# A two-layer graph network on one core: layer two's sums in three wider products, and every 64th gather replaced by single-row loads from SP

## The chip, the cores and the metric

The kernel runs on one core of a Trainium2 chip. The core has TensorE (PE; its weight loads are shown as PEld), VectorE (DVE), ScalarE (ACT), GpSimd (POOL) and SyncE (SP), which run their own instruction streams and wait for one another through semaphores. SP, ACT and POOL also issue DMAs, which 16 DMA engines carry out. The metric is the device time of one execution in microseconds (us); lower is better. Times of single instructions come from one profiled execution.

## The reference

The inputs are 6,250 nodes with 160 features each (64 scalars and 32 three-vectors), and 200,000 edges (src, dst), sorted by dst. There are two layers, each followed by a residual and a layer norm. Cut to what matters, with constants and reshapes left out:

```
# layer one, per edge: ss, vv = features of src; e0, e1 = edge attributes (1 + 3)
out0 = ss*e0 @ W1 + dot(vv, e1) @ W2
out1 = (ss @ W3) x e1 + (vv*e0) @ W4 + cross(vv, e1) @ W5
m_agg = segment_sum(concat(out0, out1), dst)
x1 = layernorm(x + (x + relu(linear(m_agg))))

# layer two: w = relu(edge_attr_10 @ W_fc1) @ W_fc2   (192 a edge: w0 64, w1 64, w2 32, w3 32)
l0, l1 = linear(x1);  y0, y1 = l0[src], l1[src]
m0 = w0*y0*e0;  m1 = (w1*y0) x e1;  m2 = (w2*e0) x y1;  m3 = w3*dot(y1, e1)
s0..s3 = segment_sum(m0..m3, dst)
o0 = s0 @ W_l2_00 + s3 @ W_l2_10;  o1 = s1 @ W_l2_01 + s2 @ W_l2_11
x2 = layernorm(x1 + self_interaction(x1) + 0.5*(o0, o1))
```

## The kernel before, in words

**Tiles.** The edges are cut into 391 chunks of 512, a chunk into four tiles (J = 4) of 128 edges, one edge a partition. Because edges are sorted by dst, the edges of one chunk end in a window of at most W = 40 neighbouring nodes. Per chunk the kernel builds a 0/1 matrix of edges by window places (`oh`, L290) and multiplies it with the four edge attributes (`S`, L294: 128 edges x 4 tiles x 4 attributes x 40 places). A matmul of the edges' features with S then sums messages by node into a window of PSUM (`ab`), and DVE adds that window into accumulators in SBUF at a start read from a register (`add`, L356 to L378; the addition itself is L367). The accumulators are accA (4 groups of node columns) and accB (one).

**Gathers.** The features of a tile's 128 source nodes are gathered from a table in HBM by one indirect DMA of GpSimd (`gathered`, L128), four a chunk, 1,564 a layer: from x in layer one, from ytab in layer two. They land in g, a pool of GRING = 8 chunks; the first two chunks are gathered ahead into a pool of their own.

**Layer one.** ScalarE copies 32 of the features four times side by side (`repeat`, L331), and PE makes two products a tile: 128 features by the 160 columns of S (L350), and the copies by the same 160 columns (L353). When all edges of a block of 128 nodes are done (`closing`), the block is projected (L390), normed, projected again (L452, L453) and written to ytab and btab (L460, L464).

**Layer two.** `hidden` (L300, L303) makes 100 hidden values per edge from `et`, which SP loads every second chunk (L260). `message` (L314 to L326) makes the weights w in PSUM and multiplies them with the gathered features into m, 320 columns an edge. `matmuls` (L337 to L345) makes three products a tile over these columns: the first 128 by 40 columns of S, the next 128 by 160, the last 64 by 80, so 280 columns in all. They fill seven windows of `ab`, of which some are not used. `add` then takes five additions: 128 rows by 40, 64 by 120, 64 by 80, and twice 32 by 40. A finished block is projected with wc (L476), whose rows are laid out to fit the accumulators (L221 to L231), added to the base that SP loads (L469), normed and sent out by SP (L487).

**Order.** The order on every engine is the order in which the program issues it. A loop over t (L496) calls each stage for chunk t minus its lag, so for layer two:

```
stages = [(load, 0), (onehot, 1), (hidden, 1), (message, 2), (matmuls, 3), (add, 4)]
parts = [(fetch_base, 3), (project_last, 5), (residual_last, 6), (deviation, 7), (sent, 8)]
```

Layer one has load, onehot, repeat, matmuls and add, and for a finished block fetch, project, rectify, residual, deviation, normed, turned, kept, linear and written. SP's queue holds all loads and stores but the gathers, srcs and ytab: raw (edge attributes, every 32 chunks, L275), et, xt (L415), btab, base, out and, at step PREPARE = 8 of layer one, the weights. Successive DMAs of SP and ACT use eight semaphores in turn, so a DMA waits for the one eight before it.

Of the kernel before, what the change touches and what calls it, by code (L numbers as in the profile page):

```python
# [10 lines left out]
F32 = mybir.dt.float32  # L11
BF16 = mybir.dt.bfloat16
I32 = mybir.dt.int32
AF = mybir.ActivationFunctionType
ALU = mybir.AluOpType
# [8 lines left out]
J = 4  # L24
# [16 lines left out]
GRING = 8  # L41
PREPARE = 8

# [10 lines left out]
def gnn_kernel(ctx: ExitStack, tc: tile.TileContext, x, src, dst, ea, sh, avec,  # L54
# [64 lines left out]
    with tc.If(go > 0) as both:  # L119
        windowed(tc, x, srcs, rel, low, ident, iota, ahead, ea, sh, avec, *weights, out)  # L120
# [3 lines left out]

def gathered(nc, pool, srcs, table, c):
    g = pool.tile([P, J, D], F32, name="g")
    for j in range(J):
        nc.gpsimd.indirect_dma_start(out=g[:, j, :], out_offset=None, in_=table,  # L128
                                     in_offset=bass.IndirectOffsetOnAxis(ap=srcs[:, c, j:j + 1], axis=0))
    return g  # L130
# [3 lines left out]
def windowed(ctx: ExitStack, tc: tile.TileContext, x, srcs, rel, low, ident, iota, ahead, ea, sh, avec,  # L134
# [11 lines left out]
    accA = const.tile([P, 4, NW], F32, name="accA")  # L146
    accB = const.tile([P, NW], F32, name="accB")
    eps = const.tile([P, 1], F32, name="eps")
    nc.vector.memset(eps, EPS)
    zero = const.tile([P, 4], F32, name="zero")  # L150
# [9 lines left out]
    def clear(k):  # L160
        part = accA[:, k, :] if k < 4 else accB
        nc.scalar.activation(part, zero[:, 0:1].to_broadcast([P, NW]), AF.Copy)  # L162

    def prepare(wp, wpp):
# [5 lines left out]
        nc.sync.dma_start(fc2, wfc2)  # L170
# [51 lines left out]
        nc.sync.dma_start(wc[32:96, 4, 0:M0], w00)  # L222
        for r, g, i in ((0, 4, 0), (96, 4, 1), (64, 0, 2)):
            nc.sync.dma_start(wc[r:r + 32, g, vec[i]], w11)
        for i in range(3):
            nc.sync.dma_start(wc[0:M0, 1 + i, vec[i]], w01)
        for r, g in ((96, 1), (0, 0), (32, 0)):
            nc.sync.dma_start(wc[r:r + 32, g, 0:M0], w10)
        nc.vector.tensor_scalar(wc, wc, L2_SCALE, None, op0=ALU.mult)
        for r, g in ((96, 1), (0, 0), (32, 0)):  # L230
            nc.vector.tensor_scalar(wc[r:r + 32, g, 0:M0], wc[r:r + 32, g, 0:M0], INV3, None, op0=ALU.mult)  # L231

    def sums(layer, table, gp, hp, sp):
        with ExitStack() as s:
# [13 lines left out]
            G, S, SH, ET, H, M, PA, AT, RAW = {}, {}, {}, {}, {}, {}, {}, {}, {}  # L248

            def load(c):  # L250
                if layer or c not in ahead:
                    G[c] = gathered(nc, gp, srcs, table, c)
                else:
                    G[c] = ahead.pop(c)
                if c % 2 == 0 and layer:
                    n = min(2, NCH - c)
                    et = ET[c // 2] = xp.tile([P, 2, CH // 2], F32, name="et")
                    part = ea[:, c * CH:(c + n) * CH].rearrange("f (c h e) -> f c h e", c=n, h=2)
                    for r in range(2):
                        nc.sync.dma_start(et[64 * r:64 * r + 10, :n, :], part[:, :, r, :])  # L260
                if c == 0:
                    attributes(0)
                if c % 32 == 12:
                    attributes(c // 32 + 1)

# [41 lines left out]
            def message(c):  # L307

                m = M[c] = wp.tile([P, J, 320], F32, name="m")
                h = H.pop(c)  # L310
                for q in range(0, J, 2):
                    pw = pp.tile([P, 2, 192], F32, name="pw")
                    for j in range(2):
                        nc.tensor.matmul(pw[:, j, :], h[:, q + j, :], fc2, start=True, stop=True)  # L314
                    y = G[c][:, q:q + 2, :]
                    thirds = m[:, q:q + 2, 0:288].rearrange("p j (d u) -> p j d u", d=3)
                    nc.vector.tensor_tensor(  # L317
                        thirds[:, :, 0:2, 32:96], pw[:, :, 0:128].rearrange("p j (a u) -> p j a u", a=2),
                        y[:, :, None, 0:64].to_broadcast([P, 2, 2, 64]), op=ALU.mult)
                    y1 = y[:, :, 64:160].rearrange("p j (d u) -> p j d u", d=3)  # L320
                    nc.vector.tensor_tensor(  # L321
                        thirds[:, :, :, 0:32], y1,
                        pw[:, :, None, 128:160].to_broadcast([P, 2, 3, 32]), op=ALU.mult)
                    nc.vector.tensor_tensor(  # L324
                        m[:, q:q + 2, 224:320].rearrange("p j (d u) -> p j d u", d=3), y1,
                        pw[:, :, None, 160:192].to_broadcast([P, 2, 3, 32]), op=ALU.mult)  # L326
# [7 lines left out]
            def matmuls(c):  # L334
                one = S.pop(c)
                if layer:
                    t = M.pop(c)  # L337
                    ab = PA[c] = pa.tile([P, 7, W], F32, name="ab")
                    parts = [(ab[:, 4, :], slice(0, 128), slice(0, 1)),
                             (ab[:, 0:4, :], slice(128, 256), slice(0, 4)),  # L340
                             (ab[0:64, 5:7, :], slice(256, 320), slice(2, 4))]
# [14 lines left out]
            def add(c):  # L356
# [8 lines left out]
                def into(rows, k, part):  # L365
                    v = accA[rows, k, ds(at, W)] if k is not None else accB[rows, ds(at, W)]
                    nc.vector.tensor_tensor(v, v, part, op=ALU.add)  # L367

                if layer:
                    into(slice(0, 128), None, ab[:, 4, :])  # L370
                    into(slice(0, 64), slice(1, 4), ab[0:64, 1:4, :])
                    into(slice(64, 128), slice(0, 2), ab[64:128, 0:2, :])
                    for i in range(2):
                        into(slice(32 * i, 32 * i + 32), 0, ab[32 * i:32 * i + 32, 5 + i, :])
                else:
                    into(slice(0, 128), slice(0, 4), ab[:, 0:4, :])
                    for k in range(4):
                        into(slice(32 * k, 32 * k + 32), None, ab[32 * k:32 * k + 32, 4 + k, :])  # L378
# [6 lines left out]
            def projected(name, pool, weights, b):  # L385
                r = rows(b)
                po = T[name, b] = pool.tile([P, D], F32, name=name)
                for g in range(5):
                    lhs = accA[:, g, b * P:b * P + r] if g < 4 else accB[:, b * P:b * P + r]
                    nc.tensor.matmul(po[:r], lhs, weights[:, g, :], start=(g == 0), stop=(g == 4))  # L390
# [29 lines left out]
            def rectify(b):  # L420
# [3 lines left out]
                nc.scalar.activation(accA[:, :, b * P:b * P + r], zero[:, :, None].to_broadcast([P, 4, r]), AF.Copy)  # L424
                nc.scalar.activation(accB[:, b * P:b * P + r], zero[:, 0:1].to_broadcast([P, r]), AF.Copy)
# [45 lines left out]
            def project_last(b):  # L471
                r = rows(b)
                po = T["po", b] = pl_.tile([P, D], F32, name="po")
                for g in range(5):
                    lhs = accA[:, g, b * P:b * P + r] if g < 4 else accB[:, b * P:b * P + r]
# [13 lines left out]
            if layer:  # L489
                stages = [(load, 0), (onehot, 1), (hidden, 1), (message, 2), (matmuls, 3), (add, 4)]  # L490
                parts = [(fetch_base, 3), (project_last, 5), (residual_last, 6), (deviation, 7), (sent, 8)]
            else:
                stages = [(load, 0), (onehot, 1), (repeat, 1), (matmuls, 2), (add, 5)]
# [408 lines left out]
```

## Time and profile before

| | us |
|---|---|
| runs: median of 3 (lowest, highest) | 5196.45 (5195.57, 5202.86) |
| the profiled execution's own time | 4000.83 |
| its span, first to last instruction | 3999.1 |
| layer one's gathers, first to last start | 11.0 to 1979.6 |
| layer two's gathers, first to last start | 2005.9 to 3965.8 |
| busy: PE, PEld, DVE, ACT, POOL | 3469.6, 2900.8, 2516.1, 601.9, 2972.9 |
| mean granted clock of TensorE | 0.931 of full speed |

The profiled execution is much shorter than the runs; durations of instructions are from it alone. In the lines that follow, a group of instructions is named by its source line, engine, operation and tiles (out<-in), then its count, then busy time and the mean of one in ns, then the idle time of the engine before them and what ended it. A wait is put down to whatever released it last; "issue" is time in which nothing that the profile shows was waited for. A q behind an engine's name means its queue, so that SPq is the time in which SP issues a DMA. Matmuls overlap, so PE's busy share says less than the spacing of the matmuls' starts.

### The profile page before, as it was taken

How to read it: one execution, taken by the hardware profiler on the slowest of the kernel's cores; microseconds unless marked ns; L12 is line 12 of the kernel's file. 1: busy time of each engine (PE TensorE's matmuls, PEld its weight loads, DVE VectorE, ACT ScalarE, POOL GpSimd, SP SyncE). 2: the span in 40 equal slices, each digit the busy share in tenths (PEclk: the TensorE clock that was granted, in tenths of full speed). 3: DMA queues.
4: the chain of work that ended last, by engine and by line, in shares of the span. 5: the costliest groups of instructions: out<-in, count | busy, mean ns of one | idle time of the engine just before them, and what ended most of it. 6: DMA issues, size and time to landing. Idle time of an engine off the chain costs nothing.

```text
span 3999.1 us, 66393 instructions
## 1 busy us (share of the span) xinstructions
PE 3469.6 (87%) x21616; PEld 2900.8 (73%) x21617; DVE 2516.1 (63%) x8489; ACT 601.9 (15%) x1187; POOL 2972.9 (74%) x3137
## 2 busy tenths in 40 slices
PE   4777777777777777787799999999999999999999
PEld 4655655556566566665578888888888888888888
DVE  4444444444444444445567877787888888888887
ACT  3111111111111111112211111111111111111111
POOL 6777777777777777777677777777777777777775
PEclk8888888888888988889989999999999999999999
DMA  2222222222222323333222222232333333333332
GB/s 76 69 66 71 71 69 71 72 74 71 74 76 74 76 74 79 80 76 82 70 70 70 75 74 73 75 76 73 77 76 77 79 76 79 77 80 80 78 77 60
DMA packets 204128, 297.15 MB, mean 74 GB/s; under 512 B 61124, under 2 KB 150342, under 8 KB 203774
## 3 DMA queue, kind: packets, MB, share of 16 engines
q0 software_dynamic: 150144, 256.45, 26.0%
q1 hardware_dynamic: 46466, 31.56, 2.8%
q10 hardware_dynamic: 7164, 4.80, 0.4%
q8 instruction: 176, 2.88, 0.3%
q14 instruction: 178, 1.46, 0.1%
HBM read 280.57 MB, written 12.00 MB: 73 GB/s over the span
## 4 chain that ended last, share of the span: by engine, by line
PE 38%; POOL 4%; issue 4%; DVE 2%; DMA 2%; DVEq 0%; ACT 0%; ACTq 0%; POOLq 0%
PE ab L344 20%; PE pw L314 11%; PE ph L300 5%; POOL g L128 4%; DMA g<-ytab,srcs 2%; PE po L476 2%; DVE accA L367 1%; DVE S L294 0%; DVE m L317 0%; DVE oh L290 0%; DVE m L324 0%; DVE accB L367 0%; DVE m L321 0%; DVEq L367 0%; DVE sh L282 0%
## 5 line engine op out<-in xcount | busy, mean ns | idle before, releaser
L128 POOL DMA_INDIRECT g<-ytab,srcs x1564 | 1484.6, 949 | 501.6 <-issue 435.5
L128 POOL DMA_INDIRECT g<-in_x,srcs x1564 | 1484.9, 949 | 476.3 <-issue 406.2
L344 PE MATMUL ab<-S,m 128*128 128x40 f32 (+2 forms) x9384 | 1123.9, 275 | 0.1
L350 PE MATMUL ab<-S,g 128*128 128x160 f32 x3128 | 735.7, 352 | 430.1 <-DMA g<-in_x,srcs 317.4
L344 PEld LDWEIGHTS ab<-S,m 128*128 128x128 f32 (+1 forms) x9384 | 1052.8, 174 | 71.6 <-issue 67.9
L350 PEld LDWEIGHTS ab<-S,g 128*128 128x128 f32 x3128 | 529.0, 214 | 621.3 <-DMA g<-in_x,srcs 472.6
L294 DVE TENSOR_TENSOR S<-oh,sh 128x640 f32<-128x640 f32 x782 | 644.8, 825 | 365.6 <-PE ab L353 279.1
L353 PE MATMUL ab<-S,r 128*128 128x160 f32 x3128 | 660.0, 366 | 65.7 <-ACT r L331 63.2
L367 DVE TENSOR_TENSOR accA<-accA,ab 32x40 f32 (+3 forms) x1955 | 467.0, 239 | 326.1 <-ACT accA L424 177.2
L353 PEld LDWEIGHTS ab<-S,r 128*128 128x128 f32 x3128 | 551.5, 231 | 150.5 <-ACT r L331 150.1
L314 PE MATMUL pw<-fc,h 100*128 100x192 f32 x3128 | 620.2, 341 | 2.3 <-DVE m L324 2.3
L314 PEld LDWEIGHTS pw<-fc,h 100*128 100x128 f32 x3128 | 501.9, 191 | 144.3 <-issue 140.1
L317 DVE TENSOR_TENSOR m<-pw,g 128x256 f32<-128x256 f32 x782 | 328.2, 420 | 302.8 <-PE pw L314 220.7
L303 ACT ACTIVATE h<-ph 100x512 f32<-100x512 f32 x391 | 233.5, 597 | 1734.1 <-PE ph L300 1724.7
L331 ACT ACTIVATE r<-g 128x512 f32<-128x512 f32 x391 | 245.7, 629 | 1593.0 <-DMA g<-in_x,srcs 1528.1
L367 DVE TENSOR_TENSOR accB<-accB,ab 32x40 f32 (+1 forms) x1955 | 372.3, 190 | 26.0 <-ACT accB L162 5.5
L300 PE MATMUL ph<-et,fc 10*100 10x256 f32 x1564 | 267.7, 418 | 5.1 <-ACT h L303 4.2
L324 DVE TENSOR_TENSOR m<-g,pw 128x192 f32<-128x192 f32 x782 | 270.5, 346 | 0.0
L321 DVE TENSOR_TENSOR m<-g,pw 128x192 f32<-128x192 f32 x782 | 268.3, 343 | 0.0
L290 DVE TENSOR_TENSOR oh<-iota,rel 128x160 f32<-128x160 f32 x782 | 257.7, 330 | 16.9
L462 DVE SCALAR_TENSOR_TENSOR base<-pl,a_sb,z 128x160 f32<-128x160 f32 (+1 forms) x49 | 18.8, 383 | 320.1 <-ACT y L459 320.1
L300 PEld LDWEIGHTS ph<-et,fc 10*100 10x100 f32 x1564 | 99.9, 161 | 47.0 <-issue 9.2
(80 smaller groups left out, 856.2 us busy)
## 6 DMA issues: line engine op xcount, KB each, us to landing
g<-in_x,srcs POOLq DMA_INDIRECT x1564
g<-ytab,srcs POOLq DMA_INDIRECT x1564
et<-in_ea SPq DMA_DIRECT2D x390, 20.0 KB
raw<-in_sh SPq DMA_DIRECT2D x96, 64.0 KB
xt<-in_x SPq DMA_DIRECT2D x48, 80.0 KB
ytab<-y ACTq DMA_DIRECT2D x48, 80.0 KB
btab<-base SPq DMA_DIRECT2D x48, 80.0 KB
base<-btab SPq DMA_DIRECT2D x48, 80.0 KB
```

Of the source, the lines that this page charges most:

```text
L128: nc.gpsimd.indirect_dma_start(out=g[:, j, :], out_offset=None, in_=table, in_offset=bass.IndirectOffsetOnAxis(ap=srcs[:, c, j:j + 1], axi ...
L290: nc.vector.tensor_tensor(oh, iota[:, None, :].to_broadcast([P, J, W]), rel[:, c, :, None].to_broadcast([P, J, W]), op=ALU.is_equal)
L294: nc.vector.tensor_tensor(S[c], oh[:, :, None, :].to_broadcast([P, J, 4, W]), attr[:, :, :, None].to_broadcast([P, J, 4, W]), op=ALU.mult)
L300: nc.tensor.matmul(ph[:, r, 0:CH // 2], fc1[64 * r:64 * r + 10, :], ET[c // 2][64 * r:64 * r + 10, c % 2, :], start=True, stop=True)
L314: nc.tensor.matmul(pw[:, j, :], h[:, q + j, :], fc2, start=True, stop=True)
L317: nc.vector.tensor_tensor(thirds[:, :, 0:2, 32:96], pw[:, :, 0:128].rearrange("p j (a u) -> p j a u", a=2), y[:, :, None, 0:64].to_broadca ...
L321: nc.vector.tensor_tensor(thirds[:, :, :, 0:32], y1, pw[:, :, None, 128:160].to_broadcast([P, 2, 3, 32]), op=ALU.mult)
L324: nc.vector.tensor_tensor(m[:, q:q + 2, 224:320].rearrange("p j (d u) -> p j d u", d=3), y1, pw[:, :, None, 160:192].to_broadcast([P, 2, 3 ...
L344: nc.tensor.matmul(o, t[:, j, f], one[:, j, k, :], start=(j == 0), stop=(j == J - 1), skip_group_check=True)
L350: nc.tensor.matmul(ab[:, 0:4, :], t[:, j, 0:128], one[:, j, :, :], start=(j == 0), stop=(j == J - 1), skip_group_check=True)
L353: nc.tensor.matmul(ab[:, 4:8, :], r[:, j, :], one[:, j, :, :], start=(j == 0), stop=(j == J - 1), skip_group_check=True)
L367: nc.vector.tensor_tensor(v, v, part, op=ALU.add)
```

## The change

There are two parts.

**Layer two's products.** The 320 message columns are permuted: w1 with y0 comes first, then (at 160) w0 with y0, and the two sets of 96 stand at 64 and 224. To match this, fc2 is loaded in three pieces with its first two blocks exchanged, and wc is filled in another layout. The three products a tile are then 128 message columns by 120 columns of S (attributes 1 to 3), 128 by 80 (attributes 0 and 3), and 64 by 40 (attribute 0), 240 in all, and fill five windows exactly. accA and accB become one tile acc with five groups, and one addition of 128 rows by 200 takes the place of five. Layer one keeps its five additions; rectify clears with one instruction instead of two.

**Rows by SP.** In every sixteenth chunk (15, 31, ... 383) POOL issues three gathers instead of four. The last tile of that chunk is loaded by SP, one DMA for each of its 128 rows. `fetch_rows` runs first in every step t: it loads eight node numbers into SP's registers and issues eight row loads of 640 bytes for the single chunk of its group of 16 steps. `numbers` loads the 128 node numbers into one partition, half a group ahead. `place_rows` has ScalarE copy the finished tile into g at lag 1, ahead of onehot. GRING falls from 8 to 7.

```
-GRING = 8
+GRING = 7
+EVERY = 16
+ROWS = -(-P // EVERY)
...
+def single(c):
+    return c % EVERY == EVERY - 1
...
 def gathered(nc, pool, srcs, table, c):
     g = pool.tile([P, J, D], F32, name="g")
-    for j in range(J):
+    for j in range(J - 1 if single(c) else J):
         nc.gpsimd.indirect_dma_start(out=g[:, j, :], out_offset=None, in_=table,
...
-    accA = const.tile([P, 4, NW], F32, name="accA")
-    accB = const.tile([P, NW], F32, name="accB")
+    acc = const.tile([P, 5, NW], F32, name="acc")
...
-        nc.sync.dma_start(fc2, wfc2)
+        for i, f in enumerate((64, 0)):
+            nc.sync.dma_start(fc2[:, 64 * i:64 * i + 64], wfc2[:, f:f + 64])
+        nc.sync.dma_start(fc2[:, 128:192], wfc2[:, 128:192])
...
+            def numbers(c):
+                if c < NCH:
+                    NUM[c] = hp.tile([1, P], I32, name="num")
+                    nc.sync.dma_start(NUM[c], src[:, c, J - 1:J].rearrange("p a -> a p"))
+
+            def fetch_rows(t):
+                c = t - t % EVERY + EVERY - 1
+                if c >= NCH:
+                    return
+                if t == 0:
+                    numbers(c)
+                if t % EVERY == 0:
+                    ROW[c] = hp.tile([P, D], F32, name="row")
+                if t % EVERY == EVERY // 2:
+                    numbers(c + EVERY)
+                a, b = t % EVERY * ROWS, min(P, t % EVERY * ROWS + ROWS)
+                _, at = nc.values_load_multi_w_load_instructions(
+                    NUM[c][0:1, a:b], engines=[mybir.EngineType.SP], min_val=0, max_val=N - 1,
+                    skip_runtime_bounds_check_because="node numbers")
+                for i in range(a, b):
+                    nc.sync.dma_start(ROW[c][i:i + 1, :], table[ds(at[i - a], 1), :])
+
+            def place_rows(c):
+                if single(c):
+                    del NUM[c]
+                    nc.scalar.activation(G[c][:, J - 1, :], ROW.pop(c), AF.Copy)
...
-                    thirds = m[:, q:q + 2, 0:288].rearrange("p j (d u) -> p j d u", d=3)
+                    mq = m[:, q:q + 2, :]
                     nc.vector.tensor_tensor(
-                        thirds[:, :, 0:2, 32:96], pw[:, :, 0:128].rearrange("p j (a u) -> p j a u", a=2),
+                        mq.rearrange("p j (a u) -> p j a u", a=2)[:, :, :, 0:64],
+                        pw[:, :, 0:128].rearrange("p j (a u) -> p j a u", a=2),
                         y[:, :, None, 0:64].to_broadcast([P, 2, 2, 64]), op=ALU.mult)
...
-                    ab = PA[c] = pa.tile([P, 7, W], F32, name="ab")
-                    parts = [(ab[:, 4, :], slice(0, 128), slice(0, 1)),
-                             (ab[:, 0:4, :], slice(128, 256), slice(0, 4)),
-                             (ab[0:64, 5:7, :], slice(256, 320), slice(2, 4))]
+                    ab = PA[c] = pa.tile([P, 5, W], F32, name="ab")
+                    parts = [(ab[:, 0:3, :], slice(0, 128), slice(1, 4)),
+                             (ab[:, 3:5, :], slice(128, 256), slice(0, 4, 3)),
+                             (ab[64:128, 4, :], slice(256, 320), slice(0, 1))]
...
-                    into(slice(0, 128), None, ab[:, 4, :])
-                    into(slice(0, 64), slice(1, 4), ab[0:64, 1:4, :])
-                    into(slice(64, 128), slice(0, 2), ab[64:128, 0:2, :])
-                    for i in range(2):
-                        into(slice(32 * i, 32 * i + 32), 0, ab[32 * i:32 * i + 32, 5 + i, :])
+                    into(slice(0, 128), slice(0, 5), ab)
...
-                stages = [(load, 0), (onehot, 1), (hidden, 1), (message, 2), (matmuls, 3), (add, 4)]
+                stages = [(fetch_rows, 0), (load, 0), (place_rows, 1), (onehot, 1), (hidden, 1), (message, 2), (matmuls, 3), (add, 4)]
...
-                stages = [(load, 0), (onehot, 1), (repeat, 1), (matmuls, 2), (add, 5)]
+                stages = [(fetch_rows, 0), (load, 0), (place_rows, 1), (onehot, 1), (repeat, 1), (matmuls, 2), (add, 5)]
```

## The prediction

> **What bounds the kernel now.** I read the two stages first, then GpSimd's waits, then the groups with shapes kept apart, then single chunks of the timeline. First, busy time by engine in a stretch of layer one and one of layer two (columns: the stretch, its length, then PE, PEld, DVE, ACT and POOL busy with instruction counts, granted clock, DMA share, GB/s):
>
> ```profile
> 100.00:1900.00 1800.00, 1372.84 (x6451) 1086.04 (x6450) 829.81 (x2784) 298.52 (x654) 1362.22 (x1438) 0.87 0.29 74
> 2200.00:3900.00 1700.00, 1689.30 (x12563) 1470.05 (x12562) 1368.22 (x4609) 209.10 (x380) 1286.83 (x1357) 0.99 0.31 77
> ```
>
> The reader should see that POOL's rate is the same in both: 1800/1438 and 1700/1357 are 1.252 and 1.253 us a gather, although PE has a quarter of its time free in layer one and 11 us in 1700 in layer two. The 16 DMA engines are 30% busy, so bandwidth binds nothing. Next, whom POOL waits for (total us, times, longest):
>
> ```profile
> POOL g L128 <- issue: 841.6, 2681, 25.3
> POOL g L128 <- PE ab L353: 36.9, 121, 0.3
> POOL g L128 <- PE ab L350: 26.2, 86, 0.3
> ```
>
> "issue" is no wait for anybody: 841.6/2681 is 0.31 us, the ordinary space between two gathers, and the "waits" for PE are just as long. So POOL never waits for a buffer. In the trace the gathers start 1.251 us apart by median, from 11.0 to 1979.6 us and from 2005.9 to 3965.8 us; the one hole is the 26 us between the layers. A chunk of four gathers takes 5.00 us, whatever the rest does. Then layer two's own work:
>
> ```profile
> L344 PE MATMUL ab<-S,m 128*128 128x160 f32 x3128 | 527.0, 312 | 0.0
> L344 PE MATMUL ab<-S,m 128*128 128x40 f32 x3128 | 388.6, 273 | 0.1
> L344 PE MATMUL ab<-S,m 128*64 128x80 f32 x3128 | 302.5, 240 | 0.0
> L367 DVE TENSOR_TENSOR accA<-accA,ab 64x120 f32 x391 | 103.2, 264 | 0.1
> L367 DVE TENSOR_TENSOR accA<-accA,ab 128x160 f32 x391 | 122.7, 314 | 306.9 <-ACT accA L424 177.2 <-PE ph L390 119.8 <-ACT accA L162 7.8
> ```
>
> PE is nearly a second bound there. With everything ready it needs 4.784 us a chunk (median spacing of the first L314 matmul), plus about 0.16 us for the projections; that is 4.94 against POOL's 5.00. Late in layer two it lags some 15 us behind the gathers, and this lag is part of the 32 us between POOL's last gather and the end. Last, what one queue issue costs SP:
>
> ```profile
> 3027.57 0.67 SPq L260 DMA_DIRECT2D et<-in_ea  x2
> 3028.29 1.73 SPq L275 DMA_DIRECT2D raw<-in_sh  x4
> 3030.11 0.68 SPq L260 DMA_DIRECT2D et<-in_ea  x2
> 3030.84 0.35 SPq L469 DMA_DIRECT2D base<-btab  x1
> ```
>
> Each issue holds SP for 0.33 to 0.43 us, with some 0.045 us between two. Now SP has little to do; after the change it has much.
>
> **The change, part by part.**
>
> *Gathers removed.* Chunks 15, 31, ... 383 have three gathers instead of four: 24 a layer, 48 in all, x 1.251 us = 60.0 us of the bound engine (a chunk falls from 5.00 to 4.93 us on average). They lie on the path, since POOL never waits. A rule speaks against counting this: the Trainium skill's page "DMA: Bandwidth & Descriptors", section "Issuing engines are not separate DMA queues", says that spreading DMAs over issuing engines saves only the sequencer's issue time, usually small beside the DMA. By that rule the move is worth about 0. By the rows the issue time is exactly the bound, with DMA engines 30% busy; I take 60.0 us.
>
> *Rows added on SP.* 6,144 DMAs of one row, eight a chunk in both layers, each behind a register operation; and before each eight a register load. No row of the trace shows a one-row DMA with an address from a register. The nearest by number of rows is et (20 short rows, median 0.325 us), then raw (32 rows, median 0.419). A register operation is 0.076 us (DVE's at L367), a load 0.463 us (SP's at L117). With 0.045 us between each: a row is 0.325 + 0.076 + 0.09 = 0.49 us, eight are 3.93, with the load 4.45 us a chunk. Added to that, each chunk: raw, xt, btab (or base, out) and the numbers, 0.19 us; in layer two also et, two issues every second chunk, 0.37. So 4.64 us in layer one and 5.00 in layer two. The ends: with 0.25 us a DMA (the shortest issues are 0.255 to 0.28) 4.0 and 4.4; with 0.419, 5.4 and 5.75. A gain below nothing is excluded, because SP's work only grows. I take 4.64 and 5.00, by the nearest row. Against a budget of 4.93 layer one fits and layer two is over by 0.07 us, 27 us in 391 chunks. That is the closest figure in this sum.
>
> *What waits for SP.* SP issues in program order. A late row makes et, base and out late behind it. place_rows makes ACT wait for the 128 rows, and behind it on ACT stand repeat or hidden of the same chunk; PE needs these one stage later. So a lag of SP up to a stage costs nothing, and a lag that grows is paid in full. At the start the numbers and eight rows come before raw: about 7 us (two loads, 2 us of landing, eight rows) until the first S. POOL has a ring of nine chunks to fill then (45 us), so I cost this at nothing. With GRING 7 the cover is 5 us smaller; in layer one PE follows a gather within 1.5 us, in layer two within 15 us, well under 35 us. ACT gains 48 copies of 128x160 (nearest, L459: 0.378 us): 18 us of an engine 15% busy, nothing. The split of fc2 into three loads and the permuted message columns leave shapes as they are: nothing.
>
> *Matmuls.* In single chunks of layer two the L344 matmuls start 112 ns apart at 40 columns, 136 at 160 and 69 at 80 (64 weight columns), each tile in two passes: 8 x (112 + 136 + 69) = 2.54 us. At 112 the weight load of 128 columns is the limit. With 120, 80 and 40 columns: 8 x (112 + 112 + 58), 58 being half of a 128-column load, = 2.26 us. PE saves 0.28 us a chunk, 109 us in all, beside POOL's bound; PE falls to about 4.66 us with projections. What reaches the end is only the lag at the tail, some 15 us.
>
> *A slower clock.* The Trainium skill's page "TensorE: Matmul & The Clock Gate", section "HAM oscillation — how this bites in real kernels", has the clock fall to half only after idle gaps over about 3.4 us. In layer one the longest waits of PE for a gather are 2.3 us, and its granted clock is 0.87. So row and rule differ. By the rule layer two stays near 1.0; by the row 5% more idle time could bring it to 0.87, and 4.66/0.87 = 5.36 would exceed 4.93. But PE would then be busy throughout, where the clock is 0.99. I take nothing, and keep 0 to 15 us for the tail.
>
> *Additions.* Five of 1.07 us together become one of 128x200, 0.36 us (314 ns at 160 columns, 1.06 ns for each further one). DVE saves 0.7 us a chunk in layer two, where it is 80% busy and PE waits for it 2.3 us in total: nothing.
>
> **Sum** in the profiled execution: -60 for POOL, -15 for the tail, +27 for SP in layer two: about -48 with SP at its estimate, -75 if SP keeps up, and a loss at SP's upper end (the first rival). I take -60, between the first two: 4000.83 to 3941, a factor of 0.985.
>
> **The runs.** The profiled execution took 4000.83 us (span 3999.1 and 1.7 around it), the median of the three runs is 5196.45, which is 1.299 times that, and they agree within 7.3 us. Nothing in the profile shows these 1196 us. If they stretch the gathers, one takes 1.66 us, a chunk 6.64, and SP has room even at 5.75. If they are a constant, the saving is 60 of 5196. If they are a half clock of PE in layer two (two chunks at about 2150 us run at half clock and take 8.9 us instead of 4.8), PE binds there. I scale: 5196.45 x 0.985 = 5118.
>
> **The rivals.**
>
> *SP becomes the bound (slower).* Mechanism: SP's chunk exceeds POOL's, in layer two first, where et stands behind the rows. At the profiled pace the loss equals the gain at 5.12 us a chunk, a row DMA of only 0.34 us. At 0.419 us: 391 x (5.75 - 4.93) + 391 x (5.4 - 4.93) = 504 us, less 75, so +430; half of that way, +140 to +200. For it: raw's 0.419, and the wait of every DMA for the one eight before it. Against: et's 0.325, and the pace of the runs, where 5.75 fits in 6.64. About 5335, between 5210 and 5600.
>
> *PE binds in the runs (faster by more).* At half clock the saving doubles to 0.56 us a chunk; over 391 chunks 219 us: about 4980. For it: half clock makes a chunk 8.9 us, and 3198 us left for layer two would be 8.2 us each. Against: layer two is granted 0.99 in the profile.
>
> *Nothing gained.* SP eats just what POOL saves: 5186 to 5207.
>
> **How the numbers follow.** POOL's saving, SP keeping up or nearly: 0.49, 5070 to 5150, likeliest 5118. PE bound: 0.11. Nothing gained: 0.06. SP bound: 0.34. About 0.2% (10 us) is what these runs can tell from no change. Faster 0.60, same 0.06, slower 0.34. The range leaves out most of the PE case (0.08) and the far part of SP's (0.12): 5020 to 5380. The likeliest case alone is 5070 to 5150.
>
> **What would show it.** Right: 3,080 gathers, still 1.25 us apart and without holes; L344 near 2.3 us a chunk; SP's eight rows and load under 4.9 us; ACT's waits at place_rows short. Wrong: gathers of POOL with waits for a buffer, ACT waiting long for row, PE waiting for et or ACT in layer two; then SP binds. A time below 5020 would mean that PE bound the runs.

## The result: 5872 us, slower by 13%

| | us |
|---|---|
| changed kernel, median of 4 runs (lowest, highest) | 5872.31 (5853.35, 5877.98) |
| kernel before beside it, median of 4 runs | 5196.20 |
| ratio, with its 95% interval | 1.1291 [1.1263, 1.132] |
| profiled execution of the changed kernel: own time, span | 5877.98, 5876.1 |
| its gathers, first to last start: layer one, layer two | 11.8 to 2981.9, 3020.4 to 5826.7 |

The forecast was 5118 us (5020 to 5380) and faster; the measured time lies above the range and on the other side. One thing has to be known to read the numbers below: the kernel before takes about 4.0 ms in the profile shown before and in set B (one chip), and 5.1 to 5.2 ms in the measured runs and in sets A, C and D (two other chips), so every ratio below compares runs on one chip.

The two stages of the changed kernel, busy time by engine (columns as before: stretch, length, then PE, PEld, DVE, ACT and POOL busy with counts, clock, DMA share, GB/s):

```profile
100.00:2900.00 2800.00, 1296.13 (x6578) 1168.58 (x6578) 849.18 (x2863) 306.25 (x650) 1366.65 (x1443) 0.70 0.19 48
3100.00:5700.00 2600.00, 2189.81 (x13419) 1913.95 (x13418) 1189.45 (x3461) 231.20 (x425) 1362.56 (x1422) 0.80 0.21 53
```

2800/1443 and 2600/1422 are 1.94 and 1.83 us a gather instead of 1.25. In layer one PE is busy for less than half of the stretch, POOL too; so a wait ends last there, and none of these engines is full. Who waits for whom (total us, times, longest), from the waits of the changed kernel:

```profile
...
ACT g L300 <- DMA row<-in_x: 938.1, 24, 59.8
POOL g L135 <- DVE acc L402: 845.8, 226, 8.7
...
PEld ab L385 <- ACT g L300: 700.0, 24, 45.0
...
DVE z L460 <- DMA xt<-in_x: 408.2, 25, 31.8
...
POOL g L135 <- ACT r L366: 276.8, 32, 35.6
...
PE ph L336 <- DMA et<-in_ea: 147.2, 49, 36.7
```

All 24 copies of `place_rows` in layer one wait, 39 us each (938.1/24), PE stands behind them (700 us), and POOL, whose ring is then full, waits for ACT (276.8 us). POOL's 845.8 us for DVE are all in layer two, and most of them do not come from the rows: at this pace the kernel before has 673.2 us of such waits (b0), and the products without rows 654.9 (mm). The lines with `xt` and `et` are loads that stand in SP's queue behind the rows. SP itself waits for little, some 80 us in layer one and 310 in layer two, most of the latter before its `out` stores (L517):

```profile
SPq L517 <- DVE oh L326: 147.6, 28, 19.7
SPq L517 <- DVE z L440: 104.0, 17, 19.7
SPq L295 <- DMA row<-ytab: 42.9, 86, 1.4
```

What SP's instructions take: L291 is the load of eight numbers, L295 the rows (count: shortest/median/longest in ns, first and last start):

```profile
L291 SPq TENSOR_LOAD <-num x768: 2/778/2552, 32.3 to 5801.8; - x192
```

```profile
L295 SPq FUSED_REGOPS  x6144: 1/37/1424, 32.9 to 5806.2; - x199
L295 SPq MOVE row<-in_x x3072: 1/29/1416, 33.0 to 2974.6; - x192
L295 SPq DMA_DIRECT2D row<-in_x x3072: 1/228/1407, 33.1 to 2974.6; - x192
```

By the medians a row is 37 + 29 + 228 ns and, with the space between, 412 ns from start to start; eight rows and the load are 4.13 us (the 5th percentile of the step, measured from the first row of one step to that of the next). The mean step is 7.67 us in layer one and 7.27 in layer two. What lies between shows in the longest column: even a register move, 29 ns by median, takes 1.4 us at times. In the timeline of the changed kernel in layer two (start, us from first to last of a group, count):

```profile
4500.61 6.17 SPq L295 DMA_DIRECT2D row<-ytab  x8
4506.88 0.68 SPq L269 DMA_DIRECT2D et<-in_ea  x2
4507.61 1.71 SPq L311 DMA_DIRECT2D raw<-in_sh  x4
4510.29 9.93 SPq L295 DMA_DIRECT2D row<-ytab  x16
```

et and raw cost what they cost before (0.68 and 1.73 us), but eight rows take 6.17 us instead of the 3.3 that eight times 412 ns make. Counted over the trace, 2,404 of SP's 20,392 instructions start 0.66 to 0.76 us after the one before; in the profile of before it was 5 of 1,090. I call such a distance a slow step. A slow step does not simply add 0.7 us, because instructions often follow at once behind it: 3,289 distances are under 0.03 us (none in unused, below, the same SP work at the 4.0 ms pace). Means are therefore the better measure. From one row's start to the next one's they give 0.83 us in layer one and 0.67 in layer two, where the medians gave 0.41. Eight rows of 0.83 and 0.76 for the load make 7.4 of layer one's 7.67 us.

Layer two's products, which answer to the L344 and L367 lines of before:

```profile
L379 PE MATMUL ab<-S,m 128*128 128x120 f32 x3128 | 544.3, 327 | 48.4 <-issue 47.7
L379 PE MATMUL ab<-S,m 128*128 128x80 f32 x3128 | 490.0, 300 | 98.8 <-issue 98.1
...
L379 PE MATMUL ab<-S,m 128*64 128x40 f32 x3128 | 299.5, 244 | 86.7 <-issue 86.5
...
L402 DVE TENSOR_TENSOR acc<-acc,ab 128x200 f32 x391 | 139.2, 356 | 3.9 <-PE po L506 2.5 <-PE ab L379 1.1 <-issue 0.3
```

The products and the one addition (356 ns, 0.36 forecast) are there as written. A gather takes 949 and 958 ns in the two layers (949 and 949 before). In layer two the rows bind less clearly than in layer one: PE is busy for 2190 of 2600 us there, `place_rows` waits 25 us in all, and PE waits 147 us for et.

### The profile page after: what moved, and what is told of

Its sections match the earlier page's. It is cut to its first block, busy times and chain, and to the rows that moved or that the text cites. A ratio compares the mean times of both kernels' runs of the same rounds, so it can differ in the third digit from the quotient of the medians.

```text
span 5876.1 us, 82733 instructions
## 1 busy us (share of the span) xinstructions
PE 3761.0 (64%) x21616; PEld 3321.9 (57%) x21617; DVE 2224.8 (38%) x6925; ACT 612.3 (10%) x1186; POOL 2940.1 (50%) x3089
## 5 line engine op out<-in xcount | busy, mean ns | idle before, releaser
L135 POOL DMA_INDIRECT g<-ytab,srcs x1540 | 1475.1, 958 | 1369.7 <-DVE acc L402 845.8
L385 PE MATMUL ab<-S,g 128*128 128x160 f32 x3128 | 662.4, 358 | 1305.0 <-ACT g L300 692.6
L379 PE MATMUL ab<-S,m 128*128 128x120 f32 (+2 forms) x9384 | 1240.8, 290 | 233.9 <-issue 232.4
L379 PEld LDWEIGHTS ab<-S,m 128*128 128x128 f32 (+1 forms) x9384 | 1210.4, 206 | 303.5 <-issue 270.5
L385 PEld LDWEIGHTS ab<-S,g 128*128 128x128 f32 x3128 | 571.4, 234 | 1374.8 <-ACT g L300 700.0
L350 PE MATMUL pw<-fc,h 100*128 100x192 f32 x3128 | 799.4, 411 | 11.4 <-DVE m L359 6.8
L350 PEld LDWEIGHTS pw<-fc,h 100*128 100x128 f32 x3128 | 648.3, 237 | 192.3 <-issue 149.6
L402 DVE TENSOR_TENSOR acc<-acc,ab 32x40 f32 (+2 forms) x2346 | 530.4, 239 | 446.3 <-ACT acc L455 173.7
L359 DVE TENSOR_TENSOR m<-g,pw 128x192 f32<-128x192 f32 x1564 | 476.0, 346 | 0.0
L336 PE MATMUL ph<-et,fc 10*100 10x256 f32 x1564 | 341.1, 488 | 189.7 <-DMA et<-in_ea 147.2
L506 PE MATMUL po<-wc,acc 128*128 128x160 f32 (+1 forms) x490 | 106.3, 379 | 47.4 <-DVE acc L402 47.3
```

What stands on the lines that cost most here:

```text
L336: nc.tensor.matmul(ph[:, r, 0:CH // 2], fc1[64 * r:64 * r + 10, :], ET[c // 2][64 * r:64 * r + 10, c % 2, :], start=True, stop=True)
L359: nc.vector.tensor_tensor(mq[:, :, f:f + 96].rearrange("p j (d u) -> p j d u", d=3), y1, pw[:, :, None, w:w + 32].to_broadcast([P, 2, 3, 3 ...
L379: nc.tensor.matmul(o, t[:, j, f], one[:, j, k, :], start=(j == 0), stop=(j == J - 1), skip_group_check=True)
L385: nc.tensor.matmul(ab[:, 0:4, :], t[:, j, 0:128], one[:, j, :, :], start=(j == 0), stop=(j == J - 1), skip_group_check=True)
```

## The experiments

The measured ratios are against the kernel before on the same chip. The last column is the time from first to last gather in layer one and layer two, from each profile; it shows where a difference sits.

| set | kernel | us | ratio [95%] | gathers, layer one / two, us |
|---|---|---|---|---|
| A, before 5084.22 | b0 | 5088.07 | 1.0003 [0.9972, 1.0034] | 2306 / 2681 |
| A | mm | 4991.62 | 0.9804 [0.9748, 0.986] | 2304 / 2589 |
| A | rows | 5908.09 | 1.1641 [1.1569, 1.1713] | 2907 / 2864 |
| A | every32 | 5106.39 | 1.0036 [1.002, 1.0051] | 2330 / 2691 |
| B, before 3996.65 | static | 3927.87 | 0.9829 [0.9806, 0.9852] | 1943 / 1932 |
| B | unused | 4064.65 | 1.0171 [1.0151, 1.0191] | 1968 / 2016 |
| B | mm7 | 3983.39 | 0.9968 [0.9957, 0.9979] | 1972 / 1961 |
| B | add5 | 3981.32 | 0.9961 [0.9946, 0.9975] | 1968 / 1955 |
| C, before 5161.4 | after2 | 5850.51 | 1.1314 [1.127, 1.1357] | 2957 / 2802 |
| C | static2 | 5105.13 | 0.9879 [0.9836, 0.9922] | 2346 / 2656 |
| C | unused2 | 5828.81 | 1.1276 [1.1227, 1.1326] | 2898 / 2820 |
| C | mm7b | 5028.66 | 0.9751 [0.9716, 0.9785] | 2316 / 2611 |
| D, before 5093.43 | oneload | 5563.42 | 1.0914 [1.0865, 1.0963] | 2723 / 2741 |
| D | static3 | 5034.31 | 0.9894 [0.9863, 0.9926] | 2319 / 2622 |
| D | after3 | 5779.73 | 1.1347 [1.1296, 1.1397] | 2913 / 2741 |

### b0: the kernel before, profiled at the slower pace

No edit.

> The kernel before, unchanged, with a profile of its own. The first profile of it took 4000.83 us, the runs 5196. Theory N (the runs have a slower pace that the first profile did not meet): this profile takes about 5196 us, and shows which engine gives the 1196 us: gathers of 1.66 us each if GpSimd is stretched, or stops of SP, DVE or GpSimd as the changed kernel's trace shows them (0.7 us each, in clusters). Rival (the first profile is what any profile of it looks like): 4000 us again, with gathers 1.251 us apart.

Measured: 5088.07 us; the profile's own time is 5089.49, 1089 us more than that of the first profile, 338 in layer one's gathers (2306 against 1969) and 721 in layer two's (2681 against 1960). Its stages and POOL's waits:

```profile
100.00:2300.00 2200.00, 1398.13 (x6733) 1204.15 (x6734) 872.32 (x2940) 318.58 (x693) 1416.86 (x1494) 0.72 0.26 63
2400.00:4900.00 2500.00, 2309.55 (x13399) 1965.61 (x13399) 1453.57 (x4920) 224.97 (x402) 1373.06 (x1449) 0.81 0.23 55
```

```profile
POOL g L128 <- issue: 1021.8, 2671, 35.8
...
POOL g L128 <- DVE m L324: 673.2, 199, 7.6
```

A chunk now takes 2306/391 = 5.90 us in layer one and 6.86 in layer two, and POOL, which waited for nobody in the first profile, waits for consumers. The durations of gathers and of DVE's operations are those of before. What is new is that matmuls come in slow steps and that the granted clock is lower (0.72 and 0.81, against 0.87 and 0.99): 369 of 21,616 start 0.66 to 0.76 us after the one before and 272 after twice that (1.33 to 1.48), against 54 and 7 in the first profile. In the second stretch PE is busy for 2310 of 2500 us and waits 53 us for DVE and 8 for ACT. So where the kernel takes 5.1 ms PE sets layer two and GpSimd no longer does.

### mm, mm7, mm7b and add5: the products without the rows

mm is the changed kernel with POOL's four gathers in every chunk and the ring of eight; mm7 and mm7b have the ring of seven; add5 is mm with the addition cut in five:

```
 GRING = 8                                  # mm, add5; mm7 and mm7b keep 7
 def single(c):
-    return c % EVERY == EVERY - 1
+    return False
...
-stages = [(fetch_rows, 0), (load, 0), (place_rows, 1), ...
+stages = [(load, 0), ...
```

```
-                    into(slice(0, 128), slice(0, 5), ab)
+                    for k in range(5):
+                        into(slice(0, 128), k, ab[:, k, :])
```

> Layer two's three products and one addition alone: four gathers in every chunk, no rows by SP, ring of 8. Theory R (SP's rows cost the 676 us): at or a little below the kernel before, 5080 to 5200 us in the runs, since PE saves 0.28 us a chunk in layer two. Rival P (the new products or the one addition slow layer two): 5500 to 5900 us, with layer two as long as in the changed kernel (2,870 us).

> Layer two's products and one addition without rows, with the ring of 7 instead of 8 gathers. It tells how much of the single chunk every 32 steps (5106 us against 4992) is the ring. If the ring matters: 5050 to 5100 us. If the rows themselves cost: within 0.4% of 4992.

> The three new products kept, ring of 8, no rows; the one addition of 128x200 cut into five of 128x40 (0.94 us instead of 0.36 of DVE, with five register operations). If the gain of the products' part (5084 to 4992 us) is PE's 0.28 us a chunk: 4980 to 5010 us. If it is DVE's single addition, which frees the windows and the ring earlier: 5040 to 5090 us.

> The products and the one addition without rows, ring of 7. On a chip at 5,100 to 5,200 us for the kernel before, where a ring of 8 gave 0.980 of it: if the ring matters, 0.99 to 1.00; if not, 0.978 to 0.985. On a chip at 4,000 us: 0.997 again.

Measured: at the pace of 5.1 ms the products alone gain 2.0% (mm, 93 us, more than the expected 5080 to 5200 us allow) and 2.5% (mm7b, 133 us, on another chip); at 4.0 ms they gain 0.3% (mm7, 13 us) to 0.4% (add5, 15 us). The windows of mm show that the gain is in layer two, where more chunks pass (13,853 matmuls in 2500 us instead of 13,399):

```profile
100.00:2300.00 2200.00, 1403.45 (x6720) 1213.56 (x6721) 869.83 (x2932) 313.13 (x644) 1421.69 (x1495) 0.72 0.26 63
2400.00:4900.00 2500.00, 2223.91 (x13853) 1910.80 (x13853) 1237.94 (x3591) 233.18 (x417) 1438.34 (x1501) 0.82 0.24 57
```

What follows: PE's saving counts only where PE is the bound; at 4.0 ms what is left is about the 15 us of tail that the prediction gave it (from the last gather's start to the end of the span 33.3 us before, 19.5 in mm7). The forecast of PE's saving was good: in mm7 the matmuls of 120, 80 and 40 columns start 112, 112 and 59 ns apart by median (112, 112 and 58 forecast), and a chunk's first L350 matmuls are 4.44 us apart where L314's were 4.78. Five additions in place of one change nothing at 4.0 ms (0.9961 against 0.9968). At 5.1 ms this was not run, so that the gain there is PE's and not the single addition's is argued from the traces: layer two gains 92 us, and in b0 PE waited for DVE only 53. The ring of seven costs nothing that shows at either pace. The first part of the change is therefore a gain in every set that has it, and the loss is the second part's.

### rows: the rows without the products

The kernel before with `single`, `numbers`, `fetch_rows`, `place_rows` and GRING = 7 of the change; the products and additions are those of before.

> Rows by SP alone: the products and additions of before, ring of 7, the last tile of every sixteenth chunk loaded row by row. Theory R: as slow as the changed kernel or slower, 5850 to 5950 us, with SP's steps at 7 us and more. Rival P: near the kernel before, 5150 to 5300 us.

Measured: 1.1641, 824 us, so theory R holds and rival P falls. The rows alone lose more than the whole change does in any set (1.129 to 1.135); the products give some of the loss back. Between the two profiled executions, rows and b0, 777 us apart, 601 us are in layer one (2907 against 2306).

### every32: half of the rows a step

```
-EVERY = 16
+EVERY = 32
```

Each step issues four rows instead of eight, and half as many gathers are replaced.

> The changed kernel with a single chunk every 32 instead of every 16, so four rows a step instead of eight (3,072 rows instead of 6,144). Theory R with SP as the bound: a step of SP falls from 7.4 to about 4.5 us, less than POOL's 4.97, so the kernel comes back to the kernel before or below it, 5000 to 5250 us. Rival (a cost for each row, wherever it lies, without a bound): half of the loss stays, 5500 to 5560 us. Rival P: unchanged, 5850 us.

Measured: 1.0036, back at the kernel before and 2.3% above mm. Halving SP's rows takes away almost all of the loss and not half of it. That is how a queue behaves which has become the bound: below the other engines' pace it costs little. The 2.3% against mm lie in layer two (2691 against 2589 us) and are not explained: the ring is not their cause (mm7b), and PE waits only 12 us for et. SP now waits again for others, 637.6 us before its `out` stores alone:

```profile
SPq L517 <- DVE oh L326: 637.6, 37, 24.8
```

### static, static2, static3: rows from fixed addresses

The rows that are loaded are then not those of the edges; the register load, the register operations and the moves are left out.

```
-                if t == 0:
-                    numbers(c)
...
-                if t % EVERY == EVERY // 2:
-                    numbers(c + EVERY)
-                a, b = ...
-                _, at = nc.values_load_multi_w_load_instructions(NUM[c][0:1, a:b], ...)
                 for i in range(a, b):
-                    nc.sync.dma_start(ROW[c][i:i + 1, :], table[ds(at[i - a], 1), :])
+                    nc.sync.dma_start(ROW[c][i:i + 1, :], table[i:i + 1, :])
...
-                    del NUM[c]
```

> The changed kernel with the 6,144 row loads kept, each from a fixed row of the table instead of the edge's own: the loads of node numbers, the register operations and moves in front of each row are left out, so the rows are not those of the edges. SP then issues 8 instructions a step for the rows instead of 25. Theory I (SP is slowed by the number of its instructions, of which many come only one in 0.7 us): SP's step falls well under POOL's 4.97 us even with such stops, and the time comes back to 5000 to 5150 us. Rival D (the row DMAs themselves, or their landing, are slow): still 5700 us or more.

> The kernel with row loads from fixed rows again (the node numbers, register operations and moves left out, so the rows are not those of the edges), beside the changed kernel on one chip. On a chip at 5,100 to 5,200 us for the kernel before: theory I (SP is slow by the number of its instructions) 4,950 to 5,150 us; rival D (the row DMAs themselves) 5,600 us or more. On a chip at 4,000 us: 3,930 us again.

> The changed kernel with the rows taken from fixed addresses: no number loads, register operations or moves on SP, and not the rows of the edges' source nodes; eight DMAs a step stay. Run as the other end of the scale for the kernel with one load. Where the kernel before takes 5.1 to 5.2 ms, theory I and rival L both expect 0.98 to 0.99; where it takes 4.0 ms, 0.98.

Measured: 0.9829 at 4.0 ms (69 us gained), 0.9879 and 0.9894 at the slower pace. All 6,144 row DMAs and their traffic are still there and ACT still copies the rows, so they are not what costs 13%, and rival D falls; theory I stands. ACT's wait for the rows of layer one falls from 952.2 us (after2) to 267.5 (static2). In static2 SP has 7,240 instructions instead of 20,392 and 1,045 slow steps instead of 2,388 (after2), and it waits for others as it does before the change:

```profile
SPq L509 <- DVE oh L318: 769.8, 41, 25.4
```

At 4.0 ms the 69 us are close to the prediction's 75 for an SP that keeps up. At the slower pace the rows do not help even so: static2 takes 76 us more than mm7b. That the 48 gathers are no longer on the path there explains why nothing is gained; what costs the 76 us was not tried.

### unused, unused2: all of SP's work, but nobody waits for the rows

```
 def gathered(nc, pool, srcs, table, c):
-    for j in range(J - 1 if single(c) else J):
+    for j in range(J):
...
-stages = [(fetch_rows, 0), (load, 0), (place_rows, 1), ...
+stages = [(fetch_rows, 0), (load, 0), ...
```

> The changed kernel with all SP work kept, but all tiles gathered by POOL as before, and the rows that SP loads not copied and not used by anybody. Theory W (engines wait for the rows): layer one comes back to about 2,320 us (2,980 in the changed kernel), while layer two, where et stands behind the rows in SP's queue, stays at 2,700 us or more. Rival C (the row traffic slows the other engines without a wait): both layers stay as long as in the changed kernel. Rival E (only the copy's wait counts, et is early enough): both come back, 5000 to 5100 us.

> All SP work kept, all four gathers kept, the rows not copied and not used by anybody, beside the changed kernel on one chip. On a chip at 5,100 to 5,200 us for the kernel before: theory W (the engines wait for SP's late rows in layer one, for et in layer two): layer one about 2,320 us, layer two 2,700 us or more, in sum 5,100 to 5,450. Rival C (the row traffic slows the other engines without a wait): 5,850 us. On a chip at 4,000 us: 4,065 us again.

Measured: unused2 loses as much as the changed kernel on the same chip (1.1276 against 1.1314). The wait has only changed its place, from the rows to the loads that SP issues behind them:

```profile
DVE z L460 <- DMA xt<-in_x: 1012.8, 45, 49.5
...
PE ph L336 <- DMA et<-in_ea: 166.3, 46, 37.5
```

So the copy in `place_rows` is not the cause; whoever needs anything from SP's queue waits. Theory W as it was put, that layer one would come back, was wrong, because `xt` stands in that queue too. The time is the one that rival C named, 5,850 us. Its mechanism, row traffic that slows the engines without a wait, is ruled out by static2, which keeps the traffic and loses nothing, and by the waits above. Rival E falls.

At 4.0 ms, unused shows SP's work without slow steps (8 of 20,348 instructions): a step is 4.13 us at its 5th percentile, as in the changed kernel, and on average 5.04 in layer one and 5.22 in layer two. Layer one keeps its length (1968), layer two grows by 56 us against before (2016 against 1960). Part of this is waits that SP has itself. From 2050 to 4000 us of this profile, SP's waits for what it stores:

```profile
SPq L517 <- DVE oh L326: 114.2, 32, 10.4
SPq L517 <- DVE z L440: 27.0, 11, 4.6
```

Before the change little stood behind a store that waits for DVE; now the rows do. How much of the 56 us this makes was not tried.

### after2, after3 and oneload: which of SP's instructions

oneload loads eight numbers once a layer and uses them in every step, so that each row keeps its register operation, its move and its DMA:

```
-                if t % EVERY == EVERY // 2:
-                    numbers(c + EVERY)
...
-                _, at = nc.values_load_multi_w_load_instructions(NUM[c][0:1, a:b], ...)
+                if t == 0:
+                    _, FIRST[0] = nc.values_load_multi_w_load_instructions(NUM[c][0:1, a:b], ...)
+                at = FIRST[0]
```

> The changed kernel, unchanged, beside its variants on one chip. On a chip where the kernel before takes about 4,000 us and no instruction stream stops (theory I): SP's step is about 4.2 to 5 us, the rows arrive in time, and the time is 3,930 to 3,990 us, faster than before by 0.3 to 1.7%. On a chip where it takes about 5,100 to 5,200 us: 5,850 us again. Rival (SP binds on every chip): slower by 5% or more on either.

> The changed kernel. Where the kernel before takes 5.1 to 5.2 ms, 1.13 of it again. Where it takes 4.0 ms: the prediction's sum gives 0.98 to 0.985 (SP keeps up at 4.1 to 4.6 us a step); the kernel whose fetched rows nobody used came out at 1.017 there, with 5.18 us a step of SP in layer two, so that theory B (SP is the bound of layer two even without slow steps) expects 1.015 to 1.03.

> The changed kernel, but each layer loads only the first eight node numbers into SP's registers and every step of that layer uses these eight for its row loads (so it fetches other rows than the changed kernel in all but the first step). SP has 24 instructions for rows in a step instead of 25: eight register operations, eight moves, eight DMAs; the load of the numbers and its wait are gone. Where the kernel before takes 5.1 to 5.2 ms: theory I (SP's slow steps of about 0.7 us fall on its instructions by their number) expects 1.10 to 1.13 of the kernel before, with over 2,000 steps of 0.66 to 0.76 us on SP. Rival L (the load of eight numbers, 0.78 us and the wait for its landing, is what stretches a step) expects it near the kernel with fixed addresses, 0.98 to 1.00. Where the kernel before takes 4.0 ms: both expect 0.98 to 1.00, since a step then needs 8 x 0.41 = 3.3 us.

Measured: after2 and after3 repeat the result (1.1314, 1.1347). oneload stands at 1.0914, a little below the 1.10 to 1.13 expected by the number of instructions and far from the 0.98 to 1.00 of rival L. In set D the way from fixed addresses to the changed kernel is 5779.73 - 5034.31 = 745 us; 529 of these come with the 16 register operations and moves a step and the addresses from registers, 216 with the load and its wait. By the profiles, which are 188 us apart, what the load costs lies in layer one alone (2913 against 2723); layer two is 2741 in both. oneload fetches the same eight rows of the table all through a layer and is slow, so the fixed rows of static3 are not fast because they are always the same. The slow steps go with the number of instructions: 927 of 7,240 in static3 (12.8%), 2,444 of 19,534 in oneload (12.5%), 2,263 of 20,392 in after3 (11.1%). What stays together in this test is the row's own three instructions: whether the two small ones or the register address of the DMA behind them matter more was not tried, nor was a kernel with as many idle instructions in their place.

No run of the changed kernel itself was at the 4.0 ms pace. Its nearest neighbours there are unused (SP's full work, 1.017) and static (SP keeps up, 0.983); what it does itself stays open.

## Why the prediction was wrong

**The step that failed: SP's time a chunk.** The prediction took 4.45 us for eight rows and the load, and 4.64 and 5.00 us a chunk with the rest. Without slow steps this was good, in part by luck: 4.13 us for rows and load, a row 0.41 instead of 0.49, the load 0.78 instead of 0.46, and three instructions a row where the sum has two (it leaves out the move). The size that was missing is the slow steps, which the sum did not contain. A row took 0.83 us in layer one and 0.67 in layer two, and a chunk 7.67 and 7.27. That SP sets this pace is shown for layer one: `place_rows` waits 938 us for rows, SP some 80 us for others, and without the register instructions the time comes back. For layer two it is shown less well, since oneload, without the load, has the same length there. The first rival, SP becomes the bound, has come true, with its mechanism (loads behind the rows are late, POOL then waits for a buffer) and by the sign it named (`place_rows`, et). Its largest price, 5.4 and 5.75 us a chunk, was still too small.

**The argument that carried the wrong side.** "The pace of the runs, where 5.75 fits in 6.64": the prediction took the 1196 us between profile and runs as room for SP. They were the opposite. On PE they come as slow steps and a lower granted clock, and the same slow steps fall on SP as soon as it has many instructions. Whoever cannot explain the difference between a profile and its runs must not book it as cover for another engine. The three readings offered for it were wrong or half right: a gather still takes 0.95 us, so nothing stretched it; it is no constant, since layer two grows by 721 us and layer one by 338; the granted clock does fall, far from half (0.72 and 0.81 by layer in b0, against 0.87 and 0.99), but it comes together with the slow steps, and the runs do not part the two.

**The layer.** The prediction let SP bind in layer two first. At the measured pace layer two takes 6.86 us a chunk before the change, so that a step of 7.27 adds little, while layer one takes 5.90 and gets 7.67. Of the 777 us between the profiles of rows and b0, 601 are in layer one. At 4.0 ms the order is as predicted (unused: layer two alone grows, by 56 us where the sum had 27).

**What SP waits for.** The prediction asked who waits for SP, not what SP waits for. Its `out` stores wait for DVE, 147.6 + 104.0 us in the changed kernel, and rows queue behind them.

**Right, at the 4.0 ms pace and with SP's register work left out.** POOL's bound, 48 gathers and the tail: 75 us forecast with SP keeping up, 69 measured (static), of which the products alone give 13 (mm7) where 15 were given to the tail. In static's profile the gathers' stretches are 26 and 28 us shorter than before, where 30 a layer were forecast. One addition instead of five: nothing, as said. GRING 7: nothing, as said. The clock: nearly nothing, as said; with PE's lighter load layer two is granted 0.97 in mm7, against 0.99 before.

**Right in part, in the runs.** "PE binds in the runs" holds for the kernel before: the products alone bring 93 to 133 us there, where the rival had 219 by assuming half clock throughout. It was counted as a rival to the SP case. They are two effects of one state: PE's saving of 2 to 2.5% is in the result, hidden by SP's loss of some 16% (rows).

**The version to keep** is the first part of the change without the second: mm or mm7, 0.975 to 0.980 of the kernel before at the slower pace and 0.997 at the faster. Beside the changed kernel on one chip it ran at the slower pace alone (set C, 5028.66 against 5850.51 us).

## What to carry to other kernels

When work moves to a queue, count its instructions as well as their durations: rows whose address came through 16 small register instructions a step, 0.03 to 0.04 us each by median, made most of a loss of 745 us, and eight DMAs a step with fixed addresses cost little (static2 takes 1.5% more than mm7b). An in-order queue that already carries loads for other stages passes its lateness to all of them, so compare its whole step, with its own waits, to the pace of each layer separately. And if the runs are 30% longer than the profile, find out in which instructions the 30% lie before counting on them.

## What the runs showed of the hardware

The kernel before takes 3997 us in set B and 5084 to 5196 elsewhere, and the durations of its gathers are the same (949 ns in the first profile, 950 and 948 in b0). In the longer executions PE and SP, when they have many instructions, fall at times into slow steps of about 0.70 us, or twice that, from one instruction to the next, register moves of 29 ns included. On SP the steps of 0.66 to 0.76 us are 11 to 17% of its instructions in every kernel with rows (2,388 of 20,392 in after2, 1,045 of 7,240 in static2, 1,907 of 11,105 in every32), 14 of 1,090 in b0, where it issues only now and then, and 8 of 20,348 in unused at the 4.0 ms pace.

One suspect is the supply of instructions. The traces list the DMA packets that bring instructions in, and they do not bear it out. For unused at 4.0 ms and then unused2 at the slower pace, which are the same kernel, the lines are (queue: packets, MB, share of the DMA engines' time):

```profile
q8 instruction: 176, 2.88, 0.3%
q14 instruction: 305, 2.50, 0.2%
...
q8 instruction: 176, 2.88, 0.2%
q14 instruction: 305, 2.50, 0.1%
```

So these packets are neither more nor slower there, and unused2 has 2,930 steps of once or twice 0.70 us on SP alone for 481 of them. Why the pace differs between chips, or between times, stays open.
